# TensorE takes columns of the copied tiles in the first layer of a graph network

## The chip, the cores and the metric

One core of a Trainium2 chip runs the whole kernel. The metric is device time in microseconds, the median over three runs. Each core has five engines with queues of their own: TensorE (PE, with its weight loads shown as PEld), VectorE (DVE), ScalarE (ACT), GpSimd (POOL) and SyncE (SP). They meet only in semaphores. Work within a queue goes in order.

## The reference

Two graph layers over 12,500 nodes of 128 features and 200,000 edges, sorted by target. Cut to what matters:

```
h = relu(layernorm(x))
x = x + segment_sum(h[src], dst) @ W_rel.T + b_rel + h @ W_root.T      # first layer
h = relu(layernorm(x))
w = silu(edge_attr @ We1 + be1) @ We2 + be2                             # one row for each edge
agg = segment_sum(h[src] * w, dst)
x = x + h + silu(agg @ Wn1 + bn1) @ Wn2 + bn2                           # second layer
```

All of it is fp32. The costly part is `h[src]`: 200,000 rows of 512 bytes in each layer.

## The kernel before

Edges go in 196 groups (`NG`) of up to eight tiles (`GT`) of 128 edges. `fetch` gathers a group's rows into one of six buffers `hs`, a tile with each indirect DMA that POOL issues (L265). `compare` makes a group's one-hot `oh` on VectorE (L278): which of 128 consecutive targets an edge goes to. `scatter` multiplies the tiles of `hs` by `oh` and sums them in PSUM (L391), and `add` adds the result to the window of targets in `both` (L409). `both` has two halves of 12,800 columns, one node a column: in each layer one half holds the features of all nodes, transposed, and the other takes the sums.

Because the features lie on the chip, a tile need not be gathered. In a *copied tile* each of its 128 edges is a column of `both`, and the columns are copied one at a time into a 128x128 tile `hc` (three buffers). The address of each column is a register: `take` loads up to 16 of them at once from `help_at` (L591), and `put` copies the columns, on VectorE as a bitwise or with zero (L606), on ACT as a copy (L608). `HELP` says how many tiles are copied in how many groups, `HC` where the tile is split between VectorE (below) and ACT (from there on); `chunks` gives each engine its part of a group. When both have done, `turn` transposes the tile on TensorE (L633) into half of a PSUM pair (`tp`) in the first layer, and `place` copies it on ACT (L639) into the last tile of `hs` of a group four later (`HW`), for which `fetch` issues one gather less. In the first layer that begins with group 18, after all features are on the chip, and takes one tile a group: 172 tiles. In the second layer nine tiles go in ten groups.

The order of every queue is written out by hand. The loop over the groups issues `fetch` of the next group, `compare` of the next, `add` of the last, `scatter`, then what `plan` put beside this group (node work, turns and placements), then `spread`, the column copies of the group. A turn stands in the group after its columns, a placement one group later.

Node work runs in batches of 512 nodes, each once all of its edges are summed, which is about every eighth group. `node_sum` multiplies by the root and relation weights (L471, L475), VectorE adds x (L483) and takes the statistics (L289, L292), and ACT takes a square root (L294), all beside one group; normalizing, storing, turning and sending to the other half follow beside the next five.

`hidden` makes the edge weights' first product in the second layer, for a whole group (L355) in the PSUM pair `hp_b`, followed by Silu on ACT (L358). Those of the first two groups stand near the end of the first layer, beside group 189.

Of the kernel before, what the change touches and what calls it, by code (L numbers as in the profile page):

```python
# [19 lines left out]
P = 128  # L20
D = 128
GT = 8
# [9 lines left out]
XB = 4  # L32
FB = 4
EP = 51
HELP = ((1, 1), (9, 10))
HC = (60, 56)
HW = 4
TABLE = 16512
HL = 16
# [27 lines left out]
def helped(n_nodes, n_edges):  # L67

    ng = n_edges // GE
    nbt = len(last_groups(n_nodes, n_edges))
    layers = []
    for begin, (tiles, groups) in ((min(ng, -(-nbt // 2) + FB) + 1, HELP[0]), (1, HELP[1])):
        ends = (begin - 1 - -(i + 1) * groups // tiles for i in range(ng * tiles // groups))
        layers.append((begin, [(e + HW, e) for e in ends if e + HW < ng - 1]))
    return layers


# [21 lines left out]
def kernel(  # L102
# [41 lines left out]
    FG = min(NG, -(-NBT // 2) + FB)  # L144
    places, blocks = help_places(N, n_edges)
    helps = [
        (layer, h, e, begin, j)
        for layer, (begin, groups) in enumerate(helped(N, n_edges))
        for j, (h, e) in enumerate(groups)
    ]  # L150
    helped_groups = {(layer, h) for layer, h, *_ in helps}

    def rows_of(ap, n0, rows, nt):
        return ap[n0 : n0 + rows * nt, :].rearrange("(t p) d -> p t d", p=rows)
# [36 lines left out]
    with (  # L191
# [42 lines left out]
        def inc(ins, sem, by=1):  # L234

            if sem not in sems:
                sems[sem], counts[sem] = tc.alloc_semaphore(f"s_{sem}"), 0
            ins.then_inc(sems[sem], by)
            counts[sem] += by
            return sem, counts[sem]  # L240
# [15 lines left out]
        def fetch(layer, g):  # L256

            k = layer * NG + g
            at(G, done["src", 0 if g < 8 else 1], done.get(("ap", k - (HB if g < NG - 8 else LB))))
            if layer:  # L260
                at(G, *(done["h1 out", b] for b in range(max(0, NBT - 2), NBT)))
            elif g >= FG:
                at(G, *(done["h0 out", b] for b in range(max(0, NBT - 3), NBT)))
            for t in range(tiles_of[g] - ((layer, g) in helped_groups)):
                ins = G.indirect_dma_start(  # L265
                    out=hs[k % HB][:, t, :], out_offset=None,
                    in_=h1_d if layer else x if g < FG else h0_d,
                    in_offset=bass.IndirectOffsetOnAxis(
                        ap=src_sb[:, g * GT + t : g * GT + t + 1], axis=0
                    ),  # L270
                )
                done["hs", k] = inc(ins, f"hs{k % HB}", 16)
# [76 lines left out]
        def hidden(g):  # L349
            n = tiles_of[g] * P  # L350
            at(T, done["ef", g // EG], done.get(("hid", g - 1)), done["const"])
            e = ef[g // EG % 2][:EF, g % EG * GE : (g % EG + 1) * GE]
            for c in range(0, n, WG):
                m = min(WG, n - c)
                ins = T.matmul(hp_b[:, c : c + m], we1_sb, e[:, c : c + m], start=True, stop=True)  # L355
            done["hp", g] = inc(ins, "pe")
            at(A, done["hp", g], done.get(("wp", g - 2)), done["help"])
            ins = A.activation(hid[g % 2][:, :n], hp_b[:, :n], AF.Silu, bias=be1_sb)  # L358
            done["hid", g] = inc(ins, "act")
# [216 lines left out]

        def chunks(layer, g, engine):

            first, last = (0, HC[layer]) if engine is V else (HC[layer], P)
            for i, begin, end in shares.get((layer, g), ()):  # L580
                lo, hi = (first + round((last - first) * share / 4) * 4 for share in (begin, end))
                for c in range(lo, hi, HL):
                    yield i, c, min(c + HL, hi)

        def take(engine, chunk):

            i, lo, hi = chunk
            at(engine, done["help"])
            kind = mybir.EngineType.DVE if engine is V else mybir.EngineType.Activation
            row, block = places[i]  # L590
            _, columns = nc.values_load_multi_w_load_instructions(  # L591
                help_at[row : row + 1, block, lo:hi], engines=[kind],
                min_val=TABLE, max_val=TABLE + 4 * (NW * WG + N - 1),
                skip_runtime_bounds_check_because="sources are nodes",
            )
            return chunk, columns

        def put(engine, taken):
# [10 lines left out]
            done["columns", i, engine is V] = inc(ins, "dve" if engine is V else "act")  # L609
            done["columns"] = [done.get(("columns", i, kind)) for kind in (True, False)]  # L610

        def spread(layer, g):

            for taken in hooked:
                put(V, taken)
            hooked.clear()
            for engine, rest in ((V, hooks), (A, list(chunks(layer, g, A)))):
                for chunk in rest or (chunks(layer, g, V) if engine is V and not layer else ()):
                    put(engine, take(engine, chunk))
            hooks.clear()  # L620

        hooks, hooked = [], []

# [8 lines left out]
            at(T, done["b3"] if layer else done.get(("placed", i - 2)), done["table", NBT - 1])  # L632
            done["tile", i] = inc(T.transpose(bank, hc[i % 3], ident), "pe")  # L633

        def place(i, layer, h):
            bank = b3[:, :P] if layer else tp[i % 2][:, 0, :]
            k = layer * NG + h
            at(A, done["tile", i], done.get(("ap", k - HB)))
            done["hx", k] = done["placed", i] = inc(A.copy(hs[k % HB][:, GT - 1, :], bank), "act")  # L639
            if layer:  # L640
                done["b3"] = done["placed", i]

        with tc.tile_critical():
# [88 lines left out]
            def plan(layer, g, what):  # L732
                beside[layer].setdefault(min(max(g, 0), NG), []).append(what)
# [19 lines left out]
                plan(0, -(-NBT // 2) + 1, lambda b=b: node_load(b))  # L753
            for b in range(min(2, NBT)):
                plan(1, ready[0] - 1, lambda b=b: node_load(b, keep_d))
            for i, (layer, h, e, begin, j) in enumerate(helps):
                tiles, groups = HELP[layer]
                for g in range(begin, e + 1):
                    lo, hi = (min(max((g + d - begin) * tiles / groups - j, 0), 1) for d in (0, 1))
                    if lo < hi:  # L760
                        shares.setdefault((layer, g), []).append((i, lo, hi))
                plan(layer, e + 1, lambda i=i, layer=layer: turn(i, layer))
                if not layer:
                    plan(0, e + 2, lambda i=i, h=h: place(i, 0, h))
            placed = {e + 1: (i, 1, h) for i, (layer, h, e, *_) in enumerate(helps) if layer}
            plan(0, FG, check_a)
            plan(0, FG + 1, check_b)
            for g in range(0, min(2 * EG, NG), EG):
                plan(0, max(NG - 8, FG + 2), lambda g=g: load(g))
            for g in range(min(2, NG)):  # L770
                plan(0, max(NG - 7, FG + 2), lambda g=g: hidden(g))

            nothing = (lambda: None, lambda: None)
            for layer in range(2):
                fetch(layer, 0)
                if layer:
                    weigh(0)
                else:
                    done["oh", 0] = inc(compare(0, 0), "dve")
                for g in range(NG):  # L780
                    k = layer * NG + g
                    if g + 1 < NG:
                        fetch(layer, g + 1)
                    if not layer:
                        if g + 1 < NG:
                            compared = compare(0, g + 1)
                            if not g:
                                done["oh", 1] = inc(compared, "dve")
                        if g < FG:
                            if 2 * g < NBT:  # L790
                                push(node_first(2 * g))
                            for c in range(-(-tiles_of[g] // NB)):
                                push(norm(g, c))
                            push(node_first(2 * g + 1) if 2 * g + 1 < NBT else nothing)
                        if g:
                            done["oh", k + 1] = add(0, g - 1)
                        scatter(0, g)
                    else:
                        if g:
                            add(1, g - 1)  # L800
                        if 2 * EG <= g + 3 < NG and (g + 3) % EG == 0:
                            load(g + 3)
                        if g + 2 < NG:
                            hidden(g + 2)
                        scatter(1, g)
                        hooks.extend(chunks(1, g, V))
                        if g + 1 < NG:
                            weigh(g + 1)
                    for what in beside[layer].get(g, ()):
                        what()  # L810
                    spread(layer, g)
                    if layer and g in placed:
                        place(*placed[g])
                add(layer, NG - 1)
                for what in beside[layer].get(NG, ()):
                    what()
# [191 lines left out]
```

## Time and profile before

| | us |
|---|---|
| median of three runs (lowest, highest) | 4920.62 (4913.62, 4926.87) |
| profiled execution | 4865.67 |
| its span, first to last instruction | 4863.9 |
| first layer's steady part, in the profile | about 300 to 2300 |
| second layer, in the profile | about 2380 to the end |

The profiled execution is 1.1% shorter than the median of the other runs. The page gives the busy time of each engine, the granted TensorE clock, the chain of work that ended last, and the costliest groups. In that chain, "issue" is time in which an engine waited for nothing that the profile shows. A small copy's duration (190 ns for L608, 150 ns for L606) is longer than its pitch, since the next one starts before it ends. fp32 products run as two passes, each with a weight load, so a product counts twice; a turn is one pass.

### The profile page before, as it was taken

The page shows a single profiled execution, that of the slowest core. Times are in us where ns is not written, and L with a number is a line of the kernel's source. Part 1 is how long each engine was busy: PE and PEld are TensorE (multiplying, and loading weights), DVE is VectorE, ACT ScalarE, POOL GpSimd, SP SyncE. Part 2 cuts the span into 40 slices and gives each one's busy share as a digit, 9 for nine tenths or more (in the row PEclk, how much of TensorE's full clock was granted, in tenths as well). Part 3 has the DMA queues.
Part 4 walks back from the last instruction along what each step waited for, and adds up shares of the span by engine and source line. Part 5 has one row for each costly group of instructions (what it writes and reads, how often), then busy time and mean ns, then how long its engine had stood idle before and what let it go on. Part 6 is the DMA issues. An engine that isn't in the chain of part 4 may idle for free.

```text
span 4863.9 us, 77667 instructions
## 1 busy us (share of the span) xinstructions
PE 2554.6 (53%) x11440; PEld 1986.8 (41%) x11440; DVE 2750.9 (57%) x21943; ACT 3051.0 (63%) x24975; POOL 2629.1 (54%) x2791
## 2 busy tenths in 40 slices
PE   2433333333333333334456767677666776667777
PEld 1423333332332333333344545455444554444555
DVE  3545555555455555555256566666655665666665
ACT  4646656666666666667356666666666666666664
POOL 6655555555555555554555455555554555555544
PEclk9666655566556666656677777777777777777778
DMA  3411111111111111111122222212221222222221
GB/s 109 112 49 50 51 43 47 47 52 46 44 45 53 45 45 53 47 47 43 52 63 58 59 62 63 59 55 61 64 58 55 59 61 59 63 61 61 58 57 48
DMA packets 187106, 275.72 MB, mean 57 GB/s; under 512 B 48331, under 2 KB 136658, under 8 KB 181586
## 3 DMA queue, kind: packets, MB, share of 16 engines
q0 software_dynamic: 89088, 182.63, 14.5%
q1 hardware_dynamic: 97300, 87.96, 5.9%
q14 instruction: 429, 3.51, 0.2%
q8 instruction: 93, 1.52, 0.1%
q10 hardware_dynamic: 196, 0.09, 0.0%
HBM read 244.89 MB, written 25.60 MB: 56 GB/s over the span
## 4 chain that ended last, share of the span: by engine, by line
ACT 33%; issue 28%; DVE 16%; PE 11%; another core or an unknown queue 8%; ACTq 3%; DVEq 1%; SPq 0%; DMA 0%
ACT hc L608 28%; DVE hc L606 9%; PE bank L391 4%; ACT hid L358 3%; PE pair L355 3%; ACTq L591 3%; DVE oh L278 2%; PE pair L368 2%; DVEq L591 1%; DVE stn L289 1%; ACT hs L639 1%; PE bank L475 1%; DVE st L289 0%; DVE hs L380 0%
## 5 line engine op out<-in xcount | busy, mean ns | idle before, releaser
L265 POOL DMA_INDIRECT hs<-h_d,src_sb x2648 | 2499.4, 944 | 2137.2 <-PE bank L391 1119.3
L608 ACT COPY hc<-both 128x4 uint8 x23936 | 2596.6, 190 | 1364.9 <-issue 1344.9
L606 DVE TENSOR_TENSOR hc<-both,bank 128x4 uint8<-128x4 uint8 x19840 | 1588.2, 150 | 1238.9 <-issue 1226.3
L391 PE MATMUL bank<-oh,hs 128*128 128x128 f32 x6252 | 1268.7, 386 | 291.1 <-issue 120.1
L391 PEld LDWEIGHTS bank<-oh,hs 128*128 128x128 f32 x6252 | 1194.4, 294 | 525.5 <-issue 264.2
L633 PE MATMUL pair<-ident,hc 128*128 128x128 f32 x172 | 73.0, 424 | 1281.1 <-ACT hc L608 411.5
L355 PE MATMUL pair<-ef,we_sb 50*128 50x512 f32 (+1 forms) x782 | 549.8, 837 | 75.8 <-ACT hid L358 33.5
L633 PEld LDWEIGHTS pair<-ident,hc 128*128 128x128 f32 x172 | 30.4, 176 | 1318.9 <-issue 778.5
L278 DVE TENSOR_TENSOR oh<-bank,rel 128x1024 f32<-128x1024 f32 x392 | 475.0, 1212 | 16.9 <-issue 16.7
L376 DVE TENSOR_TENSOR pair<-pair,be_sb 128x1024 f32<-128x1024 f32 x196 | 240.3, 1226 | 407.6 <-PE pair L368 214.9
L368 PE MATMUL pair<-we_sb,hid 128*128 128x128 f32 x3126 | 441.6, 302 | 4.7 <-issue 4.7
L368 PEld LDWEIGHTS pair<-we_sb,hid 128*128 128x128 f32 x3126 | 434.9, 222 | 3.0 <-issue 3.0
L358 ACT ACTIVATE hid<-pair,be_sb 128x1024 f32<-128x1024 f32 x196 | 217.1, 1108 | 105.5 <-remote 58.9
L355 PEld LDWEIGHTS pair<-ef,we_sb 50*128 50x128 f32 x782 | 172.7, 244 | 260.2 <-issue 222.4
L380 DVE TENSOR_TENSOR hs<-pair,hs 128x1024 f32<-128x1024 f32 x196 | 239.3, 1221 | 17.6 <-DMA hs<-h_d,src_sb 8.1
L633 PE MATMUL bank<-ident,hc 128*128 128x128 f32 x170 | 58.6, 345 | 353.6 <-remote 87.1
L633 PEld LDWEIGHTS bank<-ident,hc 128*128 128x128 f32 x170 | 26.2, 154 | 391.6 <-issue 137.9
L265 POOL DMA_INDIRECT hs<-in_x,src_sb x136 | 128.5, 945 | 73.2 <-issue 40.2
L409 DVE TENSOR_TENSOR both<-both,bank 128x128 f32 x392 | 109.0, 278 | 71.8 <-remote 47.1
L483 DVE TENSOR_TENSOR bank<-bank,xt 128x512 f32<-128x512 f32 (+1 forms) x25 | 17.2, 689 | 153.7 <-PE bank L475 52.9
L294 ACT ACTIVATE sdn<-mvn,eps 128x4 f32<-128x4 f32 (+1 forms) x50 | 14.9, 298 | 125.0 <-DVE mvn L292 45.6
L555 PE MATMUL bank<-bn_r,ones_r 1*128 1x512 f32 (+1 forms) x50 | 37.8, 845 | 90.0 <-remote 60.7
(69 smaller groups left out, 888.9 us busy)
## 6 DMA issues: line engine op xcount, KB each, us to landing
hs<-h_d,src_sb POOLq DMA_INDIRECT x2648
ef<-in_ef_t SPq DMA_DIRECT2D x98, 408.0 KB
xt<-in_x SPq DMA_DIRECT2D x48, 256.0 KB
h_d<-h SPq DMA_DIRECT2D x48, 256.0 KB
keep_d<-xt SPq DMA_DIRECT2D x24, 256.0 KB
xt<-keep_d SPq DMA_DIRECT2D x24, 256.0 KB
out_x<-xt SPq DMA_DIRECT2D x24, 256.0 KB
hs<-in_x,src_sb POOLq DMA_INDIRECT x136
```

What stands on the lines that cost most here:

```text
L265: ins = G.indirect_dma_start(out=hs[k % HB][:, t, :], out_offset=None, in_=h1_d if layer else x if g < FG else h0_d, in_offset=bass.Indire ...
L278: return V.tensor_tensor(oh[k % OB][:, :n, :], io.unsqueeze(1).to_broadcast([P, n, W]), rel[:, g, :n].unsqueeze(2).to_broadcast([P, n, W]) ...
L355: ins = T.matmul(hp_b[:, c : c + m], we1_sb, e[:, c : c + m], start=True, stop=True)
L358: ins = A.activation(hid[g % 2][:, :n], hp_b[:, :n], AF.Silu, bias=be1_sb)
L368: ins = T.matmul(wp[:, t, :], hid[g % 2][:, t * P : (t + 1) * P], we2_sb, start=True, stop=True)
L376: ins = V.tensor_add(w, w, be2_sb.unsqueeze(1).to_broadcast([P, n, D]))
L380: done["msg", g] = inc(V.tensor_mul(h, w, h), "dve")
L391: ins = T.matmul(ap[k % AB], hs[k % HB][:, t, :], oh[k % OB][:, t, :], start=(t == 0), stop=(t == tiles_of[g] - 1),)
L591: _, columns = nc.values_load_multi_w_load_instructions(help_at[row : row + 1, block, lo:hi], engines=[kind], min_val=TABLE, max_val=TABLE ...
L606: ins = V.tensor_tensor(to, column, zero_b, ALU.bitwise_or)
L608: ins = A.copy(to, column)
L633: done["tile", i] = inc(T.transpose(bank, hc[i % 3], ident), "pe")
```

## The change

`HELP` of the first layer becomes nine tiles in eight groups, 193 tiles. `HC` gets a second bound for each layer: in the first, VectorE takes columns 0 to 55, ACT 56 to 115 and TensorE 116 to 127. TensorE's columns go by `move`: the registers are loaded on its queue, and each column is multiplied by the identity into one column of a half of `hp_b`. The products stand at the end of the group, after the group's turn and before the next group's scatter. At the start of the next group's work beside, ACT copies these columns from PSUM into `hc` (`empty`). Where two tiles end in one group, both are placed in the same later group, in its last two tiles (`slot`), and that group issues six gathers. `hidden` of the second layer's first two groups moves from group 189 to 192, and waits until `hp_b` has been emptied. The second layer's shares stay: VectorE 56, ACT 72, TensorE none. The diff, cut to its core:

```
-HELP = ((1, 1), (9, 10))
-HC = (60, 56)
+HELP = ((9, 8), (9, 10))
+HC = ((56, 116), (56, 128))
...
-            for t in range(tiles_of[g] - ((layer, g) in helped_groups)):
+            for t in range(tiles_of[g] - helped_groups.count((layer, g))):
...
+            if g < 2:
+                at(T, done.get(("emptied", done.get("moved"))))
...
-            first, last = (0, HC[layer]) if engine is V else (HC[layer], P)
+            bounds = (0, *HC[layer], P)
+            first, last = bounds[(V, A, T).index(engine) :][:2]
...
+        def move(taken):
+            (i, lo, hi), columns = taken
+            n = done["moved"] = done.get("moved", 0) + 1
+            bank = hp_b[:, n % 2 * WG :][:, : hi - lo]
+            at(T, done.get(("emptied", n - 2)), *(done["table", b] for b in range(NBT)))
+            for c, place_ in enumerate(columns):
+                column = both_b[:, ds(place_ - TABLE, 4)].bitcast(F32)
+                ins = T.matmul(bank[:, c : c + 1], ident, column, start=True, stop=True)
+            moved.append((n, i, lo, hi, bank, inc(ins, "pe")))
+
+        def empty():
+            for n, i, lo, hi, bank, full in moved:
+                at(A, full, done.get(("tile", i - 3)))
+                done["emptied", n] = inc(A.copy(hc[i % 3][:, lo:hi], bank), "act")
+                done["columns", i, False] = done["emptied", n]
+                done["columns"] = [done.get(("columns", i, kind)) for kind in (True, False)]
+            moved.clear()
...
+            for chunk in chunks(layer, g, T):
+                move(take(T, chunk))
...
-            done["hx", k] = done["placed", i] = inc(A.copy(hs[k % HB][:, GT - 1, :], bank), "act")
+            done["hx", k] = done["placed", i] = inc(A.copy(hs[k % HB][:, GT - 1 - slot, :], bank), "act")
...
-                plan(0, max(NG - 7, FG + 2), lambda g=g: hidden(g))
+                plan(0, max(NG - 4, FG + 2), lambda g=g: hidden(g))
...
+                    empty()
                     for what in beside[layer].get(g, ()):
                         what()
                     spread(layer, g)
```

More of the change, by code (lines that the diff above doesn't have):

```diff
@@ L75, in helped @@
     for begin, (tiles, groups) in ((min(ng, -(-nbt // 2) + FB) + 1, HELP[0]), (1, HELP[1])):
-        ends = (begin - 1 - -(i + 1) * groups // tiles for i in range(ng * tiles // groups))
-        layers.append((begin, [(e + HW, e) for e in ends if e + HW < ng - 1]))
+        ends = [begin - 1 - -(i + 1) * groups // tiles for i in range(ng * tiles // groups)]
+        slots = [ends[:i].count(e) for i, e in enumerate(ends)]
+        layers.append((begin, [(e + HW, s, e) for s, e in zip(slots, ends) if e + HW < ng - 1]))
     return layers
@@ L146 @@
     helps = [
-        (layer, h, e, begin, j)
+        (layer, h, slot, e, begin, j)
         for layer, (begin, groups) in enumerate(helped(N, n_edges))
-        for j, (h, e) in enumerate(groups)
+        for j, (h, slot, e) in enumerate(groups)
     ]
-    helped_groups = {(layer, h) for layer, h, *_ in helps}
+    helped_groups = [(layer, h) for layer, h, *_ in helps]
     def rows_of(ap, n0, rows, nt):
@@ L588, in take @@
             at(engine, done["help"])
-            kind = mybir.EngineType.DVE if engine is V else mybir.EngineType.Activation
+            kind = engine.engine
             row, block = places[i]
@@ L610, in put @@
             done["columns"] = [done.get(("columns", i, kind)) for kind in (True, False)]
+        moved = []
+        def move(taken):
[14 more added lines that the diff above has]
+            moved.clear()
         def spread(layer, g):
@@ L633, in turn, with place @@
             done["tile", i] = inc(T.transpose(bank, hc[i % 3], ident), "pe")
-        def place(i, layer, h):
+        def place(i):
+            layer, h, slot, *_ = helps[i]
             bank = b3[:, :P] if layer else tp[i % 2][:, 0, :]
@@ L755 @@
                 plan(1, ready[0] - 1, lambda b=b: node_load(b, keep_d))
-            for i, (layer, h, e, begin, j) in enumerate(helps):
+            placed = {}
+            for i, (layer, h, _, e, begin, j) in enumerate(helps):
                 tiles, groups = HELP[layer]
@@ L762 @@
                 plan(layer, e + 1, lambda i=i, layer=layer: turn(i, layer))
-                if not layer:
-                    plan(0, e + 2, lambda i=i, h=h: place(i, 0, h))
-            placed = {e + 1: (i, 1, h) for i, (layer, h, e, *_) in enumerate(helps) if layer}
+                if layer:
+                    placed[e + 1] = i
+                else:
+                    plan(0, e + 2, lambda i=i: place(i))
             plan(0, FG, check_a)
@@ L812 @@
                     if layer and g in placed:
-                        place(*placed[g])
+                        place(placed[g])
                 add(layer, NG - 1)
@@ L969, in by_tile @@
         return np.pad(v, (0, pad), constant_values=fill).reshape(-1, P).T
-    helps = [h for _, groups in helped(a["x"].shape[0], n_edges) for h, _ in groups]
+    helps = [
+        (h + 1) * GT - 1 - slot
+        for _, groups in helped(a["x"].shape[0], n_edges)
+        for h, slot, _ in groups
+    ]
     places, blocks = help_places(a["x"].shape[0], n_edges)
     help_t = np.zeros((P, blocks[-1], P), np.int32)
-    for place, h in zip(places, helps):
-        help_t[place] = a["src"][(h + 1) * GE - P : (h + 1) * GE]
+    for place, t in zip(places, helps):
+        help_t[place] = a["src"][t * P : (t + 1) * P]
     arrays = {
```

## The prediction

> **What bounds the kernel now.** I read the page first, then the waits of the first layer's steady part (300 to 2250 us), then the copies by stretches, then one node batch on the timeline.
>
> The page's busy shares name no bound, but its chain of waits does:
>
> ```profile
> PE 2554.6 (53%) x11440; PEld 1986.8 (41%) x11440; DVE 2750.9 (57%) x21943; ACT 3051.0 (63%) x24975; POOL 2629.1 (54%) x2791
> ...
> ACT 33%; issue 28%; DVE 16%; PE 11%; another core or an unknown queue 8%; ACTq 3%; DVEq 1%; SPq 0%; DMA 0%
> ```
>
> ScalarE (ACT) and "issue" (an engine waiting for nothing that is shown) make 61% of the chain. The waits of the first layer say whose:
>
> ```profile
> POOL hs L265 <- PE bank L391: 483.0, 98, 10.1
> PE pair L633 <- ACT hc L608: 380.6, 67, 25.8
> ...
> DVE bank L483 <- PE bank L475: 45.5, 9, 10.0
> ```
>
> POOL, which gathers, waits for TensorE's scatter to free a buffer (98 times); TensorE waits at the turn L633 for ACT's column copies. So the gathers are not the bound of this layer; ACT is. Following each of the 172 copied tiles through the timeline, ACT's last column is always later than VectorE's, in the median by 4.7 us, and a tile takes 11.9 us. Why 68 columns take so long shows in ACT's copies L608 by stretches (length, busy time and count, clock, DMA):
>
> ```profile
> 1482.90:1486.60 3.70, 3.61 (x37) 0.87 0.13 38
> 1486.60:1492.80 6.20, 2.25 (x17) 0.50 0.22 54
> 1492.80:1500.20 7.40, 7.15 (x73) 0.73 0.07 18
> 1500.20:1506.65 6.45, 2.24 (x19) 0.76 0.20 52
> ```
>
> Fast stretches make 9.9 copies per us, slow ones 2.8. A slow stretch begins some 3.7 us after the first gather of a group and ends 2.4 us after the issue of the last; VectorE slows with ACT. Gathers are issued every 1.25 us. So a gather does matter to ACT, through the length of the slow stretch.
>
> Once in eight groups a node batch is summed. One of them (start, duration, engine, line):
>
> ```profile
> 1539.51 0.45 PE L633 MATMUL pair<-ident,hc 128*128 128x128 f32 x1 [12.44 <-remote]
> ...
> 1539.75 3.64 PE L391 MATMUL bank<-oh,hs 128*128 128x128 f32 x16
> ...
> 1541.92 5.14 ACT L608 COPY hc<-both 128x4 uint8 x52 [0.17 <-issue]
> ...
> 1543.32 1.26 PE L471 MATMUL bank<-b_rel_r,ones_r 1*128 1x512 f32 x2
> ...
> 1545.50 1.06 PE L475 MATMUL bank<-w_rel_sb,both 128*128 128x128 f32 x8
> ...
> 1546.60 0.70 DVE L483 TENSOR_TENSOR bank<-bank,xt 128x512 f32<-128x512 f32 x1 [4.39 <-PE bank L475]
> ...
> 1548.67 0.30 ACT L294 ACTIVATE sdn<-mvn,eps 128x4 f32<-128x4 f32 x1 [1.61 <-DVE stn L289]
> ```
>
> Turn, scatter, sum, VectorE's statistics, and then ACT's square root, for which ACT has already idled 1.61 us: here TensorE is on ACT's path. In 17 of the 22 batches of this layer TensorE has no gap from that turn to the sum's last product (the chain takes 6.6 to 9.6 us).
>
> **The change, part by part** (first layer only; the second keeps its tiles and shares). The copied tiles go from 172 to 193; VectorE's columns per tile from 60 to 56, ACT's from 68 to 60, TensorE takes 12.
>
> *ACT's columns.* 172 x 68 = 11,696 become 193 x 60 = 11,580: 116 fewer at 98 ns (68 took 6.70 us in a fast stretch): -11 us.
>
> *ACT's copies out of PSUM.* The changed order has 300 of them, 4 to 12 columns each. Floor: 98 ns, the pitch of the smallest copy; ceiling: 256 ns, the whole duration of the nearest row, L639 (128 columns, PSUM to SBUF). The next copy starts 150 ns after such an L639, and these are a tenth as wide, so 110 ns: +33 us (29 to 77).
>
> *21 more placements L639* at 150 ns: +3 us.
>
> *21 fewer gathers on POOL.* POOL itself is covered (it waits for TensorE). Each one shortens a slow stretch by 1.25 us, in which ACT makes 3.5 copies where it would make 12.4: 0.9 us, in all -19 us (0 to -26).
>
> *VectorE.* 488 more copies at 74 ns (16 in 1.19 us) and 127 more register loads with the 0.35 us gap they leave: +80 us, 0.47 us a group. Its cover: 141 us of waiting at L483 in 22 batches, 0.8 us a group, and it ends before ACT. I cost it at nothing; without the cover it is those 80 us.
>
> *TensorE's products.* 13.5 columns a group, each a register operation, then two passes of weights and product. The register operation took 57 ns on VectorE (L409). For the passes the nearest rows are the scatter's 16: 1.95 us at full clock and 3.64 at half, 0.12 to 0.23 us for weights and 128 columns together. With one column left, the pass is between half of that (weights alone) and all of it: 0.12 to 0.46 us for two passes. I take 0.25 a column with the register operation partly beside the passes: 3.4 us. The register load comes first. The rows:
>
> ```profile
> L591 ACTq TENSOR_LOAD <-help_at x1767: 305/1025/1673, 273.7 to 4815.8; - x197
> L591 DVEq TENSOR_LOAD <-help_at x1405: 342/1104/1791, 274.0 to 4809.7; - x176
> ```
>
> The median is that of 16 registers, 64 ns each, so some 0.85 us for 12. The Trainium skill (Runtime: NRT & Kernel Launch, Instruction fetch mechanics) speaks against the change here: about 200 ns for a register load, even in bulk. That would be 2.4 us, and 1.6 us more on each batch below, +26 us in the sum. It speaks of loads from HBM, these are from SBUF; the row decides. Together a group's products put 4.3 us (2.5 to 7.5) between the turn and the next scatter.
>
> *Who waits for them.* TensorE's queue is scatter, sum, turn, products, scatter. (a) In the ordinary group ACT begins the next group with the copy out of PSUM, about 5 us after the turn in TensorE's time; ACT's own group takes over 7 us in 95 of 100, so it rarely waits: +8 us for the rest. Behind that wait all of ACT's columns queue. POOL and VectorE's add also get the scatter later; POOL is five groups ahead, VectorE's add looks to the scatter before. (b) In a batch the products stand before scatter and sum, and ACT's square root comes later. In the 17 batches without a gap this is 17 x 4.3 = 73 us, less 7 us where ACT came later than the statistics anyway: 66 us. In the other five the gap takes it. Against that stands the clock: the windows show 0.50 in this scatter and 0.95 in this sum. The skill (TensorE: Matmul & The Clock Gate, Part 1) has the full clock come after some 3.4 us of busy TensorE. If one-column products count as busy, scatter and sum run at full clock: 1.4 us less in the scatter, and in the nine longer chains another 1.5; the delay is then 34 us. No row shows what such products do to the clock. I take +45 us.
>
> *The second layer's first two hidden products (L355)* move from group 189 to 192, with their two Silus and the table load on ACT, past three scatters, the last turn and placements, and two clears; their loads on SP stay. In the profile ACT sat 2.9 and 3.9 us for them before its last tile's columns. Up to 10 us are freed there; TensorE gives up to 7 back before the last sums. -4 us.
>
> Sum: -11 + 33 + 3 - 19 + 8 + 45 - 4 = +55 us on the profiled 4865.7 us, 1.1%. The median of the runs, 4920.6, lies 1.1% above the profiled execution; the same share on it gives 4976 us.
>
> **Rivals.** *The clock saves it (0.25).* Place: scatter and sum of the batches. The products warm TensorE so that a batch loses no more than 0.3 us. It decides from about 4 us saved per batch. For it: 0.95 to 1.00 once TensorE has worked for 4 us. Against: half of the sums already run warm. With the copies at their floor and the whole 10 us of the moved work: -11 + 29 + 3 - 19 + 2 + 3 - 10 = -3, 4918 us; with the gathers at -26, 4911, and little is left beyond.
>
> *TensorE becomes the bound (0.15).* A column at 0.46 us, or TensorE's issue slowed in the slow stretches as ACT's and VectorE's is: 7.5 us of products, 0.45 of turn, 3 of scatter, 0.6 of sums come to 11.5 us a group against ACT's 11.9, and ACT waits in every short group. Sums 17 x 7.5 - 7 = 120, other waits 30: +152, 5074 us. Against: the scatter's products keep their pace in slow stretches.
>
> *The gathers don't fall.* The changed order has 21 fewer on POOL, so this is out.
>
> **How the numbers follow.** The likeliest case (0.60) has 4976 us, its own range 4940 to 5035. A measurement of this kernel can tell about 0.3%, 15 us, from no change. The clock rival gives 0.15 within it, 0.08 faster, 0.02 slower; the likeliest case 0.56 slower, 0.03 within, 0.01 faster; the third 0.15 slower. Together 0.09, 0.18, 0.73. The range, 4903 to 5072, leaves out about one in ten on each side.
>
> **What would show it.** In the profile after: 2,316 x 2 TensorE passes of `both` by `ident` with some 0.12 us a pass; 300 ACT copies from `pair` of about 110 ns pitch; idle time before ACT's square root rising from some 55 us in 22 batches to about 100; slow stretches shorter in groups of six gathers. I am wrong if that idle time stays, if ACT's copies from PSUM are preceded by long waits for TensorE, or if VectorE ends tiles last.

## The result, and the profile after

The changed kernel took 5028.38 us (median of four runs, 5021.13 to 5035.53), the kernel before 4917.29 us on the same chip (4913.62 to 4926.87). The ratio is 1.0223 [1.0201, 1.0245]: slower by 2.2%, some 110 us. The prediction had 4976 us and slower as the likeliest sign; the time lies inside its range, 52 us above its middle.

Runs were made on several chips. The medians of the kernel before on them go from 4871 to 4931 us, so every ratio below is against the kernel before on the same chip, with a 95% interval. The second layer, which the change leaves alone, takes 2291 to 2380 us from its first turn to its last in the profiles, and differs most from chip to chip. I therefore read times in the first layer only, from its first turn to its last. There the profiles before and after have 2039 and 2161 us; a second profile of the kernel before had 2063. With one profile each, and from different chips, about 100 to 120 us are the first layer's: the whole loss.

The page of the changed kernel, its busy shares, its chain of waits and three of its groups:

```profile
PE 3537.3 (70%) x16093; PEld 2927.3 (58%) x16093; DVE 2796.0 (56%) x22431; ACT 3058.4 (61%) x25180; POOL 2609.5 (52%) x2770
...
ACT 37%; issue 27%; PE 14%; DVE 11%; another core or an unknown queue 7%; ACTq 3%; DVEq 1%; SPq 0%; DMA 0%
...
L627 PEld LDWEIGHTS pair<-both,ident 128*128 128x128 f32 x4632 | 922.4, 307 | 123.1 <-issue 123.0
L627 PE MATMUL pair<-both,ident 128*128 x4632 | 935.2, 335 | 82.1 <-issue 74.9
...
L296 ACT ACTIVATE sdn<-mvn,eps 128x4 f32<-128x4 f32 (+1 forms) x50 | 14.9, 298 | 177.3 <-DVE stn L291 81.6
```

TensorE has nearly 1000 us more work (53% busy became 70%), ACT as much as before, and ACT's share of the chain has risen from 33% to 37%. The change gave TensorE work and took none off the engine that carries the end. The waits of the first layer (300 to 2400 us):

```profile
POOL hs L267 <- PE bank L395: 576.2, 127, 32.1
...
PE pair L662 <- ACT hc L634: 168.7, 83, 7.5
...
ACT sdn L296 <- DVE stn L291: 70.4, 16, 6.5
...
ACT sdn L296 <- DVE mvn L294: 28.2, 5, 8.9
```

POOL still waits for the scatter, so POOL itself still isn't the bound. TensorE still waits at its turn for ACT, now for the copy out of PSUM (L634), which ends a tile. The square root's two rows had 22.0 and 23.6 us before (300 to 2250 us). The column copies by stretches (length, ACT's busy time and count, clock, DMA):

```profile
1168.27:1172.98 4.71, 3.64 (x37) 0.81 0.11 28
1172.98:1177.71 4.73, 1.75 (x16) 0.50 0.23 55
1177.71:1185.42 7.71, 7.25 (x73) 0.72 0.08 21
1185.42:1191.41 5.99, 1.54 (x9) 0.50 0.20 55
```

The second line is the slow stretch of a group with six gathers, 1.26 us shorter than that of seven in the fourth. But in that fourth line ACT made 9 copies in 6 us: over the whole first layer 2.0 copies per us in slow stretches, where the kernel before had 2.6. Nothing in the prediction's sum stands for this.

One node batch with TensorE's products behind its turn, on the timeline:

```profile
1104.29 1.16 PE L479 MATMUL bank<-w_root_sb,both 128*128 128x128 f32 x8
...
1106.09 1.88 PE L479 MATMUL bank<-w_rel_sb,both 128*128 128x128 f32 x8 [0.64 <-issue]
1106.86 0.16 ACT L634 COPY hc<-pair 128x12 f32<-128x12 f32 x1
...
1108.10 0.70 DVE L487 TENSOR_TENSOR bank<-bank,xt 128x512 f32<-128x512 f32 x1 [2.06 <-PE bank L479]
...
1110.17 0.30 ACT L296 ACTIVATE sdn<-mvn,eps 128x4 f32<-128x4 f32 x1 [3.15 <-DVE stn L291]
...
1110.76 0.45 PE L662 MATMUL pair<-ident,hc 128*128 128x128 f32 x1 [2.59 <-ACT sdn L296]
...
1111.84 5.27 PE L627 MATMUL pair<-both,ident 128*128 x24 [0.63 <-issue]
...
1116.98 3.47 PE L395 MATMUL bank<-oh,hs 128*128 128x128 f32 x16
...
1119.06 0.16 ACT L634 COPY hc<-pair 128x12 f32<-128x12 f32 x1
```

ACT has idled 3.15 us before the square root. Below it, 24 passes of one column each take 5.27 us, 0.22 us a pass; the 16 passes of the scatter under them, with 128 columns each, take 3.47 us, 0.22 as well. The granted clock was 0.50 over these products and 0.56 over this scatter. And the copy out of PSUM comes 1.9 us after the last product, since it stands at the start of ACT's next group: TensorE does not make it wait here.

### The profile page after: what moved, and what is told of

Its sections match the earlier page's. It is cut to its first block, busy times and chain, and to the rows that moved or that the text cites. A ratio compares the mean times of both kernels' runs of the same rounds, so it can differ in the third digit from the quotient of the medians.

```text
span 5033.7 us, 90407 instructions
## 1 busy us (share of the span) xinstructions
PE 3537.3 (70%) x16093; PEld 2927.3 (58%) x16093; DVE 2796.0 (56%) x22431; ACT 3058.4 (61%) x25180; POOL 2609.5 (52%) x2770
## 4 chain that ended last, share of the span: by engine, by line
ACT 37%; issue 27%; PE 14%; DVE 11%; another core or an unknown queue 7%; ACTq 3%; DVEq 1%; SPq 0%; DMA 0%
ACT hc L613 32%; DVE hc L611 5%; PE bank L395 4%; ACTq L596 3%; ACT hid L362 3%; PE pair L359 3%; PE pair L627 2%; PE pair L372 2%; DVE oh L280 1%; DVE stn L291 1%; ACT hs L669 1%; PE bank L479 1%; DVEq L596 1%; PE bank L549 1%
## 5 line engine op out<-in xcount | busy, mean ns | idle before, releaser
L611 DVE TENSOR_TENSOR hc<-both,bank 128x4 uint8<-128x4 uint8 x20328 | 1635.8, 150 | 1376.3 <-issue 1347.9
L395 PEld LDWEIGHTS bank<-oh,hs 128*128 128x128 f32 x6252 | 1233.8, 302 | 513.5 <-issue 292.8
L395 PE MATMUL bank<-oh,hs 128*128 128x128 f32 x6252 | 1322.9, 397 | 282.1 <-issue 141.4
L627 PEld LDWEIGHTS pair<-both,ident 128*128 128x128 f32 x4632 | 922.4, 307 | 123.1 <-issue 123.0
L627 PE MATMUL pair<-both,ident 128*128 x4632 | 935.2, 335 | 82.1 <-issue 74.9
L372 PE MATMUL pair<-we_sb,hid 128*128 128x128 f32 x3126 | 430.2, 296 | 4.9 <-issue 4.9
L372 PEld LDWEIGHTS pair<-we_sb,hid 128*128 128x128 f32 x3126 | 422.6, 217 | 3.4 <-issue 3.4
```

Source lines behind the costliest of these rows:

```text
L372: ins = T.matmul(wp[:, t, :], hid[g % 2][:, t * P : (t + 1) * P], we2_sb, start=True, stop=True)
L395: ins = T.matmul(ap[k % AB], hs[k % HB][:, t, :], oh[k % OB][:, t, :], start=(t == 0), stop=(t == tiles_of[g] - 1),)
L611: ins = V.tensor_tensor(to, column, zero_b, ALU.bitwise_or)
L627: ins = T.matmul(bank[:, c : c + 1], ident, column, start=True, stop=True)
```

## The experiments

First layer: from its first turn to its last. "Slow rate": ACT's column copies per us in the slow stretches, taken from 3.9 us after a group's first gather to 2.4 us after its last, and counted from the trace's records. "Root idle": ACT's idle time before the first layer's square roots. Both come from one profile each.

| run | ratio to before | first layer, us | slow rate | root idle, us |
|---|---|---|---|---|
| before (first profile) | | 2039 | 2.61 | 55 |
| after | 1.0223 [1.0201, 1.0245] | 2161 | 1.98 | 110 |
| before_again | 0.9969 [0.9940, 0.9999] | 2063 | 2.57 | 51 |
| tiles_only | 1.0187 [1.0115, 1.0258] | 2143 | 2.80 | 17 |
| share_only | 0.9776 [0.9707, 0.9845] | 1940 | 2.25 | 150 |
| gather_less | 0.9543 [0.9477, 0.9610] | 1853 | 3.08 | 53 |
| dummy | 0.9999 [0.9984, 1.0014] | 2075 | 2.31 | 86 |
| dummy_long | 0.9976 [0.9962, 0.9991] | 2068 | 2.26 | 67 |
| late_before | 1.0021 [1.0008, 1.0035] | 2067 | 2.40 | 48 |
| late_after | 1.0185 [1.0134, 1.0237] | 2144 | 1.88 | 107 |
| after_one_tile | 0.9852 [0.9810, 0.9894] | 2001 | 1.99 | 127 |
| one_tile_16 | 0.9983 [0.9972, 0.9995] | 2053 | 2.08 | 146 |
| dummy_reg | 1.0130 [1.0106, 1.0154] | 2125 | 1.91 | 109 |
| one_tile_8 | 0.9706 [0.9684, 0.9728] | 1908 | 2.36 | 113 |

before_again to gather_less shared a chip, dummy to late_after another, after_one_tile to dummy_reg a third. The slow rate moves by some 0.2 where no product was added: late_before, whose column copies are those of before, has 2.40. Whether the chip does it, or its later turns, is not shown.

**before_again**: the kernel before, unchanged.

> The kernel before, unchanged, profiled a second time beside its timings. The profile after is 170 us longer than that of before, of which the first layer has 118 us, and the second, whose code is the same, 40 us; the medians differ by only 111 us. Theory (the second layer's 40 us are chance between two executions): this profile has its first layer within 10 us of the first profile's, and its second layer is longer by 20 to 50 us. Rival (the change slows the second layer, by what it leaves behind): both layers repeat within 10 us.

It measured 0.3% under the same kernel's other runs. That is how far a ratio of that chip can be trusted beyond its interval. Both expectations missed: the first layer was 24 us longer than in the first profile, and the second 24 us shorter (2310 us against 2334). So 24 us between the layers of two profiles need no change of the kernel.

**tiles_only and share_only** divide the change into its halves. tiles_only has 193 tiles and no TensorE; share_only has TensorE's columns and the old 172 tiles.

```
 # tiles_only
-HELP = ((1, 1), (9, 10))
-HC = (60, 56)
+HELP = ((9, 8), (9, 10))
+HC = ((60, 128), (56, 128))
 # share_only
-HC = (60, 56)
+HC = ((60, 116), (56, 128))
```

> The changed kernel with its 193 tiles, but without TensorE's columns: VectorE has columns 0 to 59, ACT 60 to 127. Nothing is multiplied by the identity, nothing copied out of PSUM. ACT has 193 x 68 = 13,124 columns instead of 11,696. Theory (ACT is the bound of the first layer, and a gather fewer saves 0.9 us): 1,428 more columns at 98 ns are +140 us, 21 gathers fewer -19, 21 placements +3, the moved hidden products -4: +120 us on before, with the idle time before ACT's square root as in before (55 us). Rival (the gathers are worth more than the columns): below +60 us.

> The changed kernel with the 172 tiles of before (one a group): VectorE keeps 60 columns, ACT gives 12 of its 68 to TensorE. Theory (ACT is the bound, and TensorE's products cost it twice: in front of the sums, and by slower copies in the slow stretches): ACT loses 172 x 12 columns, -202 us, gains 172 copies out of PSUM at 55 ns, +9, waits some 50 us more before its square roots and 50 us more in the slow stretches: some -90 us on before, if TensorE with 24 passes a group does not become the bound itself. Rival (the products hold up every group): no faster than before.

tiles_only lost 1.9%, some 90 us, between the 120 of the theory and the 60 of the rival; its root idle fell to 17 us, which neither had. share_only gained 2.2%, 109 us, near the theory's 90, though its root idle rose by some 100 us instead of 50. So the extra tiles alone cost: a tile saves one gather and costs 68 columns on ACT, which bounds. TensorE's share alone is worth having, though 12 of ACT's 68 columns are 18% of them and a tile came only from about 12.0 to 11.35 us. Where the rest went is in the waits of share_only (300 to 2250 us):

```profile
PEld pair L662 <- DVE hc L611: 286.7, 143, 6.1
...
ACT sdn L296 <- DVE stn L291: 107.1, 15, 8.2
```

The turn now waits for VectorE's columns: in 134 of the 172 tiles (78%) its last column ends after ACT's copy out of PSUM, where in the kernel before it never was last. The first row is a new bound, the second the wait that was predicted.

**gather_less**: the kernel before with one gather fewer in each helped group of the first layer; the rows of that tile are left as they were in the buffer.

```
-            for t in range(tiles_of[g] - ((layer, g) in helped_groups)):
+            for t in range(tiles_of[g] - ((layer, g) in helped_groups) * (2 - layer)):
```

> The kernel before, but in the first layer each group that has a copied tile issues one gather fewer still (six for seven), and multiplies what its buffer held: 172 gathers are left out, nothing is put in their place. Theory (a gather fewer shortens the slow stretch by 1.25 us, in which ACT makes 3.5 copies for 12.4): 172 x 0.9 = -155 us. Rival (the slow stretches are not the gathers' doing, or they only move): within 30 us of before.

172 gathers fewer took 186 to 211 us off the first layer, against the two profiles of before: 1.1 to 1.2 us each, more than the 0.9 expected, where POOL issues one in 1.25. The slow stretches shrank from 1020 to 799 us. That POOL waits for TensorE and a gather still costs its whole length fits a price paid in ACT's and VectorE's slow stretches.

**dummy and dummy_long**: the kernel before, with TensorE making products behind the turns of the first layer that nobody reads. In dummy they are 14 products with one column of the identity, at a fixed address; in dummy_long three with 512 columns.

```
+            if not layer and (0, g) in shares and g < NG - 7:
+                for c in range(14):
+                    T.matmul(hp_b[:, WG + c : WG + c + 1], ident, ident[:, c : c + 1], start=True, stop=True)
 # dummy_long
+                for c in range(3):
+                    T.matmul(hp_b[:, WG:], ident, iota, start=True, stop=True)
```

> The kernel before with its tiles and shares, and 14 products of the identity with one fixed column each (28 passes, no registers, nothing waits for them, their result is not read) where the changed kernel has TensorE's columns, in the first layer. They only occupy TensorE's queue. Theory (the change loses by the place of the products in front of scatter and sum, and by what TensorE's many instructions do to the slow stretches): idle time before ACT's square root from 55 to 100 us or more, ACT's copies in the slow stretches from 2.6 to about 2.0 per us, first layer 90 to 130 us longer. Rival (the register loads and register operations on TensorE's queue slow the other engines): square root as above, but copies in the slow stretches stay at 2.6 per us, first layer some 50 us longer.

> As the one with 14 products of one column, but with three products of the identity with 512 fixed columns: TensorE is about as long at work (six passes of 0.4 to 0.9 us) with 12 instructions for 56. Theory (it is the number of TensorE's instructions that slows ACT and VectorE in the slow stretches): their rate stays near 2.6 per us, the square root waits as with the 14: first layer 40 to 60 us longer. Rival (it is TensorE's reading and its time at work): rate near 2.0, first layer 90 to 130 us longer.

All four expectations missed the time: dummy cost nothing that can be measured, though its root idle rose to 86 us, and dummy_long gained 0.2%. From the turn's end to the next scatter TensorE takes 5.6 us in dummy, 4.1 in dummy_long and 5.7 in the changed kernel (medians; the means are 4.8, 3.8 and 5.8). So TensorE's time in that place, nearly as long in dummy as with the change, makes no loss by itself, nor does a root idle of that size. ACT's idle time before column copies is 647 us in dummy and 647 in late_before on the same chip: products with a fixed address leave it as it was. Part of the root idle lies in slow stretches, where ACT would have made few copies. In dummy the batches' sums took 3.12 us (median, 5.66 in the kernel before), at a granted clock of 0.99; part of the delay is paid back there.

**late_before and late_after**: turn and placement one group later in the first layer, so that a turn finds its columns done; late_after is the changed kernel with this, with a fourth `hc`, and with one more wait before the products.

```
-                plan(layer, e + 1, lambda i=i, layer=layer: turn(i, layer))
+                plan(layer, e + (1 if layer else 2), lambda i=i, layer=layer: turn(i, layer))
...
-                    plan(0, e + 2, lambda i=i: place(i))
+                    plan(0, e + 3, lambda i=i: place(i))
```

> The kernel before with the first layer's turns and placements one group later (the turn two groups after its columns, the placement three). TensorE then no longer waits at a turn for the columns that ACT has just made, ahead of scatter and sum. Theory (the square root waits for a chain that begins at that turn): its idle time falls from 55 us to under 15, first layer some 40 us shorter. Rival (the sum waits for VectorE's add in any case): idle time over 40 us, first layer within 15 us.

> The changed kernel with the first layer's turns and placements one group later, with a fourth buffer for the copied tile. Theory: the idle time before ACT's square root falls from 110 us to under 30, the slow stretches stay at 2.0 copies per us: first layer 80 us shorter than the changed kernel's, still 20 to 50 us longer than that of before. Rival (TensorE is the bound of the first layer by now): within 20 us of the changed kernel.

Neither changed much: 1.0021, as the rival had it, with 48 us of root idle instead of under 15; and for late_after 1.0185 against the change's 1.0223, with overlapping intervals, and 17 us less in the first layer, where the theory had 80. That is the size that the rival of late_after named, but not its cause: TensorE isn't the bound there. In late_after the wait for ACT only moved from the turn to the products (L627 waited 199.6 us for L634). TensorE's wait at the turn is a symptom of a late ACT, not its cause.

**after_one_tile and one_tile_16**: the changed kernel with 172 tiles again, then with 16 columns on TensorE as well.

```
-HELP = ((9, 8), (9, 10))
+HELP = ((1, 1), (9, 10))
 # one_tile_16 also
-HC = ((56, 116), (56, 128))
+HC = ((56, 112), (56, 128))
```

> The changed kernel with one copied tile in each group again (172 tiles instead of 193); the shares stay VectorE 56, ACT 60, TensorE 12. Theory (ACT's columns pay, the extra tiles cost them back, and what TensorE's part adds in waits is the same for either ratio): against the changed kernel 21 x 60 columns fewer at 98 ns are -123 us, 21 gathers more at 1.15 us +24, placements and copies out of PSUM -5: about -104 us, a ratio to before of 1.001 (0.995 to 1.007). Rival (at nine tiles in eight groups the three engines wait for each other in turn, and at one tile a group this coupling goes as well): as good as the run with the shares 60, 56 and 12 or better, 0.965 to 0.985, idle time before ACT's square root under 150 us, and VectorE last in fewer than half of the tiles.

> As the run before, with TensorE taking 16 columns of a tile: VectorE 56, ACT 56, TensorE 16. Theory (ACT's columns pay at 98 ns each, TensorE's cost 0.41 us each on a queue with two us a group to spare): 172 x 4 ACT columns less are -67 us, and TensorE's four more columns are +1.6 us a group that come through only in the batches (22 x 1.6 = +35): 0.6% under the run with 56, 60 and 12. Rival (TensorE's products are by now what ACT waits for): equal to that run or slower, with ACT's idle time before its copies out of PSUM over 50 us.

after_one_tile gained 1.5%. From 1.0223 to 0.9852 are about 180 us for 21 tiles; my arithmetic said 104. It is the price of a column that was wrong: between the two profiles ACT makes 1250 fewer columns in the first layer, and in the fast stretches it makes 8.2 per us, with all that stands between them, not one each 98 ns. That is 152 us, less 19 for slow stretches that are 25 us longer: 133 of the 159 us between the profiles. The other 26 are hardly more than the 24 by which two profiles of the kernel before differ, so the coupling of the rival isn't needed, but it isn't refuted: 0.9852 lies at the edge of its range, though above share_only's 0.9776, and its root idle under 150 us and VectorE never last fit either theory.

one_tile_16 missed on both theories. It was 1.3% slower than after_one_tile, not faster; and ACT's idle time before its copies out of PSUM was 14 us, not over 50. What the profile shows (waits, 300 to 2250 us):

```profile
POOL hs L267 <- PE pair L662: 264.6, 54, 7.7
...
PE pair L662 <- ACT hc L634: 61.9, 35, 3.4
```

TensorE waits for ACT a quarter as long as in after_one_tile (227.7 us there), and is busy in 87% of the first layer (79% there). POOL waits for a TensorE that has become late. ACT's issue gaps before column copies rose by 60 us in the first layer, from 666 to 726. Why they rose outside the slow stretches too (7.1 copies per us there, 8.3 in after_one_tile) stays open.

**dummy_reg**: as dummy, but the products take their columns as the change does, by register: 12 of them in each of 171 groups by the trace, read from `both`, and nobody reads the results.

```
+            if not layer and (0, g) in shares and g < NG - 7:
+                _, columns = take(T, (shares[0, g][0][0], P - 12, P))
+                at(T, *(done["table", b] for b in range(NBT)))
+                for c, place_ in enumerate(columns):
+                    column = both_b[:, ds(place_ - TABLE, 4)].bitcast(F32)
+                    T.matmul(hp_b[:, WG + c : WG + c + 1], ident, column, start=True, stop=True)
```

> The kernel before, with TensorE loading 12 registers and making 12 products of the identity with the columns that they name in each of 165 groups of the first layer; nothing reads the results, and the shares of VectorE and ACT are those of before. It differs from the run with static products only in the register loads and addresses. Theory (TensorE's products cost by what waits for them behind, not by their registers): 0.998 to 1.006, idle time before ACT's square root +30 to +60 us as with the static products. Rival (register-addressed instructions of a third engine slow the issue of ACT and VectorE, which is where the changed kernel's 50 to 70 us of additional issue gaps come from): 1.010 to 1.020, ACT's issue gaps before column copies +50 us or more, copies in slow stretches at 2.0 to 2.2 per us instead of 2.6.

The rival's ratio held: 1.0130. The kernel before had the same median on the chips of both dummies (4930 and 4931 us), so they can be put side by side. ACT's column copies in all slow stretches that begin between 600 and 1800 us, first of dummy, with the first of 99 stretches and the sum (length, ACT's busy time and count, clock, DMA):

```profile
611.33:617.32 5.99, 1.84 (x14) 0.52 0.23 57
...
sum 594.38, ACT 195.91; mean ACT 1.98
```

then of dummy_reg, 97 stretches:

```profile
608.32:614.30 5.98, 1.74 (x10) 0.50 0.23 59
...
sum 580.93, ACT 168.67; mean ACT 1.74
```

ACT is busy for 33% of such a stretch in the one and 29% in the other. Over the first layer 2325 copies fell into slow stretches in dummy, 1922 in dummy_reg, in stretches of the same length (1009 and 1005 us). The 403 others had to be made outside, at 8.7 per us: 46 of the 50 us by which dummy_reg's first layer is longer. VectorE lost likewise, from 2.79 to 2.32 per us. ACT's 0.4 is twice what its rate moved by between runs without products. While the products themselves run in slow stretches, ACT and VectorE make 4.3 copies per us together in dummy_reg, and 5.6 in dummy; in the rest of these stretches 4.2 and 4.4. In the changed kernel the lower rate is in the rest (3.7, against 4.6 beside the products), so the place of the loss within a stretch is not shown.

ACT's idle time over the first layer divides these 50 us (dummy, then dummy_reg):

```profile
L608 ACT COPY hc<-both 128x4 uint8 x11628 | 1258.7, 193 | 646.9 <-issue 640.1
L294 ACT ACTIVATE sdn<-mvn,eps 128x4 f32<-128x4 f32 x22 | 6.6, 298 | 86.2 <-DVE stn L289 60.2 <-DVE mvn L292 24.6 <-issue 1.5
...
L608 ACT COPY hc<-both 128x4 uint8 x11628 | 1253.8, 190 | 677.5 <-issue 671.1
L294 ACT ACTIVATE sdn<-mvn,eps 128x4 f32<-128x4 f32 x22 | 6.5, 297 | 109.3 <-DVE stn L289 88.1 <-DVE mvn L292 17.5 <-issue 3.7
```

31 us more lie before column copies, which wait for nothing that the profile shows, and 23 before the square roots, which come later: the batches' sums took 5.66 us in dummy_reg (median), 3.12 in dummy. The rival's mark of +50 us in the issue gaps was not reached, and 25 us of such gaps separate the two profiles of the kernel before; the size of this half is therefore uncertain, and the ratio is the firmer evidence.

So taking columns by register on a third engine slows the other two, where their copies are slow already, although nothing waits for its results: the engines do not meet in semaphores alone. dummy_reg differs in more than one thing: it loads registers, each product has a register operation (85 ns in the trace), and the products read `both`, from which the other engines copy. Which of these does it was not told apart.

**one_tile_8**: fewer such products. VectorE 60, ACT 60, TensorE 8, 172 tiles.

```
-HELP = ((9, 8), (9, 10))
-HC = ((56, 116), (56, 128))
+HELP = ((1, 1), (9, 10))
+HC = ((60, 120), (56, 128))
```

> One copied tile a group, VectorE 60 columns, ACT 60, TensorE 8: between the kernel before (60, 68, 0) and the run with 60, 56, 12. Theory (each register product of TensorE takes about one column copy away from ACT and VectorE in the slow stretches, 12 of them cost 1.3%, so 5 us a column; an ACT column is worth 17 us; ACT ends last again): against 60, 56, 12 four ACT columns more are +67 us, four products fewer -21, TensorE's shorter queue in 22 batches -30: +16 us, a ratio to before of 0.981 (0.975 to 0.987), ACT and VectorE in slow stretches 2.2 and 2.9 copies per us or more, idle time before ACT's square root about 100. Rival (the products' number hardly matters, only that TensorE has some): ratio 0.988 or above, as ACT's four columns come through whole.

0.9706, the lowest ratio of the divisions, though share_only's interval just reaches it, and better than the theory's 0.981 with its range: it is the sign of the trend that holds, not the size. Its waits (300 to 2250 us):

```profile
PE pair L662 <- ACT hc L634: 293.3, 86, 8.9
...
ACT sdn L296 <- DVE stn L291: 74.0, 15, 7.6
```

TensorE waits for ACT again, so it has room; ACT ends 97% of the tiles, but only 1.3 us after VectorE (median), so the two are balanced; the slow rates are 2.36 and 3.11.

Two pairs of runs show the number of products at work where ACT's columns and tiles are the same. From one_tile_8 to after_one_tile, four columns of a tile go from VectorE to TensorE; ACT has 60 in both, and its idle time before column copies rises from 588 to 666 us, of 93 us by which the first layer is longer. From share_only to one_tile_16 ACT has 56 in both, and it rises from 626 to 726, of 113. The runs of a pair come from different chips, but 78 and 100 us are well over the 25 between the two profiles of before. The second pair is the weaker, as TensorE is late in one_tile_16.

one_tile_8 beats both kernels: 4731.75 us against 4878.73 for the kernel before on that chip, lowest and highest of its runs 4726.91 and 4738.42; the changed kernel is 2.2% above the kernel before.

## Why the prediction was right in sign and low in size

- *What bounds.* Right. ACT is last in 192 of the 193 tiles after the change, POOL and VectorE have cover left. VectorE's additional work was rightly costed at nothing at 56 columns; share_only shows what happens when ACT has 56 and VectorE 60: VectorE is last.
- *ACT's columns.* The count was right and hardly changed (116 fewer), so the price didn't matter here. As a price for other edits 98 ns was low: in the fast stretches a column goes with 113 to 124 ns (8.8 per us before, 8.1 after), everything else of ACT included.
- *Copies out of PSUM.* Predicted 110 ns of pitch, +33 us; the trace has a duration of 155 ns and, from the start of a copy to the start of the next instruction, about 55 (median): +16 us.

```profile
L634 ACT COPY hc<-pair x300: 147/155/172, 300.4 to 2461.1; 128x8 f32<-128x8 f32 x63, 128x4 f32<-128x4 f32 x44, 128x12 f32<-128x12 f32 x43
its engine sat idle before it (us, times) until:
  PE pair L627: 1.6, 3
  issue: 0.9, 2
```

- *Waits for products in the copy.* Predicted +8 us; the lines just shown have 2.5.
- *Gathers.* Predicted 0.9 us each; gather_less gives 1.1 to 1.2, so -24 us instead of -19.
- *TensorE's products.* Predicted 0.25 us a column (0.12 to 0.46) and 4.3 us a group (2.5 to 7.5) from turn to scatter. They took 0.41 and 5.8, inside the range. The middle was too low because a pass with one column costs what one with 128 costs: in dummy 28 passes of one column took 5.97 us and the 16 of the scatter behind them 3.76, 0.21 and 0.24 us each, both at a granted clock of 0.50. The load of 12 registers took 0.87 us (the first line below), as the trace of before said and not as the Trainium skill (Runtime: NRT & Kernel Launch, Instruction fetch mechanics) has it for loads from HBM, whose 200 ns a register would be 2.4 us for 12. The loads on TensorE's queue (minimum, median, maximum in ns), of 12 registers each in after_one_tile, then of 4 to 12 in the changed kernel:

```profile
L596 PEldq TENSOR_LOAD <-help_at x172: 844/867/1398, 274.9 to 2286.8; - x172
L596 PEldq TENSOR_LOAD <-help_at x300: 330/602/1487, 285.4 to 2452.7; - x150
```

- *The square root.* Predicted to idle 100 us instead of 55, and it idles 110. As idle time the predicted middle was close. As a price it is shown only in part: dummy has 86 us of it at a ratio of 1.000, against 48 in late_before on the same chip. ACT's next step in a batch (L310) idles 13 us more, which the prediction had not counted. Its "the delay is then 34 us" does not come out of its own figures, which give 66 - 17 x 1.4 - 9 x 1.5 = 29; for the +45 this makes no difference that matters.
- *The clock.* In the batch above, products run at 0.50. The Trainium skill (TensorE: Matmul & The Clock Gate, Part 1) has the full clock after some 3.4 us of busy TensorE; in the batch shown, 5.27 us of products left the scatter behind them at 0.22 us a pass, where the scatter at full clock had 0.12 in the kernel before. So the page's rule does not show here, and the measurement decides. The delay is hardly given back: the sums behind them took 5.42 us in the median after the change and 5.66 before. The rival that the clock saves it is refuted for these products. In dummy, with products at a fixed address, the sums did run at a high clock; why there and not here stays open. TensorE as the bound was refuted at 12 columns and nearly reached at 16.
- *The second layer's hidden products.* Predicted -4 us; the time between the last turn of one layer and the first of the next went from 140.9 to 145.3 us. No gain.
- *What was missing.* The step that failed is "In the ordinary group [...] it rarely waits: +8 us". It counts only what waits for the products, and that was right (2.5 us). They also slow what doesn't wait for them, for which the sum has no term. ACT's idle time over the first layer shows it (before, then after):

```profile
L608 ACT COPY hc<-both 128x4 uint8 x11628 | 1257.3, 190 | 627.3 <-issue 617.6
L294 ACT ACTIVATE sdn<-mvn,eps 128x4 f32<-128x4 f32 x22 | 6.5, 297 | 55.3 <-DVE stn L289 26.9 <-DVE mvn L292 23.6 <-issue 4.7
...
L613 ACT COPY hc<-both 128x4 uint8 x11512 | 1242.5, 191 | 697.4 <-issue 689.3
L296 ACT ACTIVATE sdn<-mvn,eps 128x4 f32<-128x4 f32 x22 | 6.5, 297 | 109.8 <-DVE stn L291 81.6 <-DVE mvn L294 28.2
```

ACT is busy for 1330 and 1332 us. Of the 122 us by which the first layer is longer, 70 are idle time before column copies and 55 before square roots; the rest of its idle time fell by 5, as the placements and hidden products lost 21 us of waits. Against before_again it is 45 and 58 of 97. So about half of the loss is the later square roots, which the prediction had in 45 us, and the other half is slower issue, which it had at nothing.

The sum with measured terms, -11 + 16 + 3 - 24 + 2.5 + 55 + 13 + 4, is +58 us against 110 measured, and slower issue is of the size of the missing 50. That this sum is so near the predicted 55 is luck: its errors, of 17 us in the copies out of PSUM against 23 in the square root and the step behind it, have opposite signs. That 5028 still lies in the likeliest case's own range, 4940 to 5035, is luck as well: half of the loss comes from something that is not among its terms. From dummy to dummy_reg the products by register cost 1.3%, some 64 us, with slower issue and later square roots in it. What makes the issue slower stays open.

So the change put two things together that pull against each other. With eight or twelve columns on TensorE and the old number of tiles, the three divisions tried gained 1.5 to 2.9%; sixteen gained nothing that counts (0.9983). The ninth tile in eight groups gave ACT that work back, for gathers that cost less than the columns.

## What to carry to other kernels

Before moving work to an idle engine, ask what that work does to the busy engines beyond waits: here their copies slowed while gathers ran, and a dummy that does the moved work without a reader prices it in one run. Don't spend what you take off the bounding engine on more work for that engine: change the division first, by itself, and measure how small a share is enough (8 of 128 columns did at least as well as 12, and better than 16). An engine's idle time names a wait, not its price.

## What the runs showed of the hardware that was not expected

- An fp32 product with one column takes as long as one with 128: 0.21 us a pass (28 passes in 5.97 us) and 0.24 (16 in 3.76), at a granted clock of 0.50 in dummy.
- TensorE, 70 to 87% busy with such register-addressed products, left its granted clock at 0.58 to 0.60 on average over the first layer, as low as in the kernel before (0.61) with 37% busy; with static one-column products and 78% (dummy) it was 0.61. With three products of 512 columns (dummy_long, 55% busy) it was 0.78.
- While gathers are under way, ACT's register-addressed copies drop from 8.8 to 2.6 per us and VectorE's from 7.0 to 3.1 in the kernel before. Where TensorE makes such products too, with the change, they drop to 2.0 and 2.3.
